# Two attention layers on a graph: the sums over keys leave TensorE, v's weights are streamed, and the order of work is rewritten

## The chip, the cores and the metric

The kernel runs on one NeuronCore of a Trainium2 chip. The metric is the device time of one execution in microseconds (us). Before the change it was 2666.83 us, the median of three runs (2666.81 to 2668.23).

The core has a matrix engine (TensorE, PE in the profile; its weight loads are PEld), three engines for elementwise work (VectorE is DVE, ScalarE is ACT, GpSimd is POOL) and a sync engine (SP), whose queue issues nearly all DMA transfers of this kernel. Each queue and each engine takes its instructions in order.

## The reference

There are 64 batches of 256 tokens with 512 features, and one 256 x 256 adjacency matrix for all. Everything is float32.

```python
# layer 0: masked attention, 8 heads of 64
q = (x @ Wq + bq).reshape(b, n, H, HD); k = (x @ Wk + bk)...; v = (x @ Wv + bv)...
scores = jnp.einsum('bqhd,bkhd->bhqk', q, k) / jnp.sqrt(jnp.float32(HD))
scores = scores + (1.0 - adj)[None, None, :, :] * -1000000000.0
attn = jax.nn.softmax(scores, axis=-1)
out = jnp.einsum('bhqk,bkhd->bqhd', attn, v).reshape(b, n, d)
x = _layernorm(x + (out @ Wo + bo), axis=-1)
# layer 1: graph attention from two projections of h
h = jnp.einsum('bnc,cf->bnf', x, W)
s1 = jnp.einsum('bnf,f->bn', h, a1); s2 = jnp.einsum('bnf,f->bn', h, a2)
e = jax.nn.leaky_relu(s1[:, :, None] + s2[:, None, :], negative_slope=ALPHA)
e = e * mask[None, :, :]                       # mask is adj
h_prime = jnp.einsum('bij,bjf->bif', jax.nn.softmax(e, axis=2), h)
x = _layernorm(x + jax.nn.elu(h_prime + beta * h), axis=-1)
```

## The kernel before, in words

**Tiling.** Batches go in pairs (`pair`, L619): 32 pairs, m = 0 to 31. A pair shares the projections q, k and v; all else is done by batch (`batch`, L702), s = 0 and 1 in the pair. A projection (`project`, L435) is done in quarters with seven products in place of eight (a Strassen scheme): the left side is a weight matrix with its sums, the right side the tokens with theirs (`token_sums`, L414, four subtractions on GpSimd). The seven products go to the PSUM tiles ps_chain, ps_cross, ps_second, ps_fourth or ps_pair, all at L455, in the order 1, 5, 2, 6, 3, 4, 7 for the wide ones.

The blocks of TensorE's work are named as the code names them, and the texts below use these names:

- **x**: transposing the input. **q, k, v**: projections of a pair, 7 products of 8 matmul records each.
- **scores** (S): per batch, 32 records on half the rows of the array, two head groups at once (ps_sc, L779). VectorE adds the mask (L786), ScalarE takes exp (L788), GpSimd adds the two key halves (L791, tile `both`), VectorE transposes in 32 x 32 blocks (L797, tile `flip`) and reduces (L798, tile `part`).
- **sums** (d): one matmul with `fold_sb` (ps_den, L806) ends the sum over keys over the partitions. Then VectorE inverts it (L809) and checks its range (L811), SP stores it to `rows` in DRAM (L815) and loads it spread over all partitions into `inv_all` (L820).
- **mix** (M): attention times v, 32 records on half the columns (ps_pv, L756); its result oT is multiplied by `inv_all` (L873).
- **o**: output projection, added to X (L951), then the norm (`norm`, L584: mean and square sums on ScalarE, three small operations on GpSimd, scaling on ScalarE, L608).
- **logits, attention**: the second layer's softmax, without TensorE for all but the last pair: dot products (L974), a transpose `svT` (L997), a store and a broadcast load (`line`, `row`, L998 and L1000), elementwise work (L1003 to L1023), a store `square` and four loads `att_b` (L1040, L1043), and a transpose (L1047) into attT.
- **spread** (y): attention times X (small products, 4 records each). **u**: projection of y, then elu, the second norm and the store of the result (`finish`, L715).

**Weights.** wq and wk are streamed (`streamed`, L380): the seven left sides are loaded for each pair, product by product, into six `piece` buffers of 256 KB. Wv, Wo and W stay in SBUF with their sums (`weight_sums`, L366, four operations on GpSimd).

**What sets the order.** The code doesn't issue instructions directly. It records operations with a cost, and `Plan.place` (L127) orders them on all engines from these costs, the lags of transfers and the number of buffers of each kind (`slots`, L258). TensorE's order is given by hand: `ROUND` lists the blocks of one round, `LATER` says how many rounds after its pair's number a block comes, and `FINISH` lists the end (`take_turn`, L612). At the end of TensorE's order the planner picks freely among the last 70 operations. A round is the work of one pair's length, with blocks of up to four pairs in it.

Of the kernel before, what the change touches and what calls it, by code (L numbers as in the profile page):

```python
# [16 lines left out]
P = 128  # L17
# [5 lines left out]
ROUND = ("v", "x", "spread1", "scores20", "scores00", "scores10", "scores30", "o1", "logits0", "q", "logits1", "u1",  # L23
         "sums0", "mix0", "scores11", "scores21", "scores01", "scores31", "attention0", "k", "spread0", "o0", "mix1",
         "sums1", "u0", "attention1")

LATER = {"x": -1, "v": 0, "spread1": 2, "scores20": 0, "scores10": 0, "scores30": 0, "scores00": 0, "o1": 1, "q": -1,
         "logits1": 1, "u1": 2, "sums0": 0, "mix0": 0, "scores11": 0, "scores21": 0, "scores01": 0, "scores31": 0,
         "attention0": 1, "k": -1, "spread0": 1, "o0": 0, "mix1": 0, "logits0": 1, "sums1": 0, "u0": 1, "attention1":
         1}  # L30

FINISH = (("scores20", 0), ("scores30", 0), ("logits0", 1), ("v", 0), ("spread1", 2), ("scores10", 0),
          ("attention0", 1), ("scores00", 0), ("u1", 2), ("o1", 1), ("sums0", 0), ("scores21", 0), ("mix0", 0),
          ("logits1", 1), ("spread0", 1), ("o0", 0), ("attention0", 0), ("spread1", 1), ("u1", 1), ("logits1", 0),
          ("attention1", 1), ("scores01", 0), ("u0", 1), ("logits0", 0), ("attention1", 0), ("spread0", 0), ("o1", 0),
          ("scores11", 0), ("u1", 0), ("sums1", 0), ("u0", 0), ("spread1", 0), ("scores31", 0), ("mix1", 0))
SAFE = 1e15

# [23 lines left out]
class Plan:  # L62
# [13 lines left out]
    SWITCH = {None: 100.0, "rows": 200.0, "columns": 100.0, "sums": 100.0, "one": 100.0}  # L76
# [50 lines left out]
    def place(self):  # L127
# [47 lines left out]
        while len(order) < len(ops):  # L175
            best = None
            for e, cand in ready.items():
# [3 lines left out]
                for n in cand:  # L181
# [18 lines left out]
                    if e == "PE" and ns:  # L200
                        cost = self.SWITCH[mode] if m != mode else self.AGAIN if start > now[e] else 0.0
# [8 lines left out]
            if e == "PE" and ns:  # L210
                start += self.SWITCH[mode] if m != mode else self.AGAIN if start > now[e] else 0.0
                mode = m
# [31 lines left out]
def gnn_two_layers(ctx: ExitStack, tc: tile.TileContext, x, adj, Wq, bq, Wk, bk, Wv, bv, Wo, bo, W, a, beta, out):  # L244
# [13 lines left out]
    slots = {"xin": 2, "x": 4, "two": 6, "xP": 1, "piece": 6, "full": 4, "half": 17, "flip": 1, "part": 1, "inv": 1,  # L258
             "xS": 2, "st": 72, "ps": 8, "rows": 4, "svT": 4, "line": 4, "square": 4}
# [37 lines left out]

    ident = const.tile([P, P], F32, name="ident")
# [19 lines left out]
    def by_partition(v, name):  # L318
        v_sb = const.tile([P, C], F32, name=name)
        with nc.allow_non_contiguous_dma(reason="one small vector, once"):  # L320
            nc.gpsimd.dma_start(v_sb, v.rearrange("(c p) -> p c", p=P))
        return v_sb

    def on_all(ap, offset, n, name):
        v_sb = const.tile([P, n], F32, name=name)
        nc.gpsimd.dma_start(v_sb, row_on_all(ap, offset, n))
        return v_sb

    wv_sb = weight(Wv, "wv_sb")
# [13 lines left out]
    fine_sb = once([32], "fine_sb")  # L343
    plan.op("POOL", 100, lambda: nc.gpsimd.memset(fine_sb[A], 1.0), [], [fine_sb])
    last_ok = st(1, "last_ok")
    fold_sb = once([32], "fold_sb")
    plan.op("DVE", 150, lambda: nc.vector.tensor_reduce(
        fold_sb[A], ident.rearrange("p (b j) -> p j b", j=32), AX.X, ALU.add), [], [fold_sb])
    maskT_sb = once([NT, N], "maskT_sb")

# [15 lines left out]
    def weight_sums(w, name, engine, reads=()):  # L366

        S = once([3, 2, F], name)
        eng, ns = (nc.vector, 700) if engine == "DVE" else (nc.gpsimd, 1300)
# [10 lines left out]
    def streamed(w, w_dram, name):  # L380
# [4 lines left out]
        for n, to, p, m, op, reads in ((1, s1, w21, w22, ALU.add, [w]), (2, s2, s1, w11, ALU.subtract, [w, S[1]]),  # L385
                                       (4, s4, w12, s2, ALU.subtract, [w, S[2]]), (3, s3, w11, w21, ALU.subtract, [w])):
            plan.op("DVE", 700, lambda to=to, p=p, m=m, op=op: nc.vector.tensor_tensor(to(), p(), m(), op), reads,  # L387
                    [S[n]])
# [25 lines left out]
    def token_sums(T, keys, name, width=P):  # L414
# [9 lines left out]
        def sub(dst, p, m, reads, writes):  # L424
            plan.op("POOL", 180 + 545 * width // P, lambda: nc.gpsimd.tensor_tensor(dst(), p(), m(), ALU.subtract),  # L425
                    reads, writes)
# [63 lines left out]
    def gather(quarter, bias=None, wide=False):  # L490

        def copy(q, acc):
# [4 lines left out]
            for f in range(2):  # L497
                plan.op("ACT", 470, lambda f=f: nc.scalar.activation(
                    dst()[:, f, :], src()[:, f, :], AF.Identity,
                    bias=bias[:, 2 * q[0] + f:2 * q[0] + f + 1]), [acc], [key])  # L500
# [37 lines left out]
    def residual_bias():  # L538
        bo_sb = for_now(bo, 0, "bo")
        acc, part = ps([D], "ps_b"), sb("half", [D], "bv_wo")  # L540
        for c in range(C):
# [3 lines left out]
                [(wo_sb, c)], [part], mode="two" if c else None)  # L545
# [10 lines left out]
    def second_layer_constants():  # L556
        plan.op("POOL", 500, lambda: nc.gpsimd.memset(diag_sb[A], 0.0), [w_sb], [diag_sb])
        for t in range(NT):
            plan.op("DVE", 250, lambda t=t: nc.vector.tensor_scalar(
                diag_sb[:, t, blk(t)], ident, beta_sb, None, ALU.mult), [], [diag_sb])  # L560
# [23 lines left out]
    def norm(X, ts):  # L584
# [10 lines left out]

        for i, t in enumerate(ts):
            total(i, t, 725, AF.Identity, mean, scale=-1.0 / D)
# [9 lines left out]
        for i, t in enumerate(ts):  # L607
            plan.op("ACT", 810, lambda i=i, t=t: nc.scalar.activation(  # L608
# [3 lines left out]
    def take_turn(m, what):  # L612
        at_end = (what, B // 2 - 1 - m) if m is not None else None
        if at_end in FINISH:
# [4 lines left out]
    def pair(m, at, general=False):  # L619
# [49 lines left out]
        right = token_sums(xT, lambda k, j: [(xT, (j, s)) for s in range(2)], "xS", N)  # L669
# [6 lines left out]
        if m == 0:  # L676
            wq_sb, wk_sb = sb("two", [C, D], "wq_sb"), sb("two", [C, D], "wk_sb")
            load(wq_sb, Wq)
            load(wk_sb, Wk)
            lq, left["q"] = streamed(wq_sb, Wq, "wq_sums")  # L680
# [3 lines left out]
            plan.turn = (plan.turn[0], plan.turn[1] + 0.5)  # L684
# [3 lines left out]
            left["v"] = weight_sums(wv_sb, "sv_sb", "POOL")  # L688
            plan.turn = (0, ROUND.index("x"))
# [7 lines left out]
        project(left["v"], right, False, [V], *gather(  # L697
# [4 lines left out]
    def batch(m, s, qT, kT, V, dram, general):  # L702
# [12 lines left out]
        def finish(ts, us, u, mode):  # L715

            for t in ts:
# [461 lines left out]
```

## Time and profile before

| | |
|---|---|
| median of three runs | 2666.83 us |
| the profiled execution, its own time | 2666.57 us |
| its span, first to last instruction | 2664.8 us |
| granted TensorE clock, mean | 0.998 |
| TensorE busy | 2643.7 us (99%) |
| VectorE, GpSimd, ScalarE busy | 1999.7, 1637.5, 1550.5 us |
| DMA | 300.70 MB, mean 113 GB/s, queue of SP 42.1% of 16 engines |

How to read the timeline's lines: start in us from the span's beginning, length, engine, line of the code, operation, output<-inputs, rows*columns of the array in use, shape, number of records; in brackets the idle time of the engine before it and what ended it. A record's length contains its way through the array, so the next one starts before it ends: durations on TensorE are taken from start to start. In the list of waits a line says who waited for whom, the total in us, the number of times, and the longest.

### The profile page before, as it was taken

What the parts mean: (1) busy time and instruction counts of PE and PEld (TensorE: products, weight loads), DVE (VectorE), ACT (ScalarE), POOL (GpSimd) and SP (SyncE); (2) the same over time, 40 slices, a digit from 0 to 9 for tenths busy, and PEclk for the clock granted to TensorE, in tenths of its full rate; (3) what the DMA queues carried; (4) which work ended last, traced back from release to release, by engine and by line L of the source; (5) the groups of instructions that cost most, each with busy time, mean ns of one, the idle gap of its engine ahead of it and who ended that gap; (6) DMA issues with size and microseconds to landing.
All of it is one profiled execution on the core that took longest, in us unless ns stands there. A gap on an engine that the chain in (4) does not pass through costs nothing.

```text
span 2664.8 us, 45965 instructions
## 1 busy us (share of the span) xinstructions
PE 2643.7 (99%) x15037; PEld 2288.5 (86%) x15037; DVE 1999.7 (75%) x4053; ACT 1550.5 (58%) x3585; POOL 1637.5 (61%) x2255
## 2 busy tenths in 40 slices
PE   9999999999999999999999999999999999999998
PEld 7888888888888888888888888888888888888886
DVE  6677787777877777777778777787777777777876
ACT  3456565555655565655656555565556565565666
POOL 4665665655756556566566565575655656656655
PEclk9999999999999999999999999999999999999999
DMA  8343443444534434444344344453443444444321
GB/s 253 83 104 111 124 127 92 114 116 112 132 95 114 116 109 124 109 108 109 112 123 127 92 113 117 113 131 96 114 117 108 125 109 106 109 113 123 96 64 53
DMA packets 583084, 300.70 MB, mean 113 GB/s; under 512 B 409400, under 2 KB 513848, under 8 KB 582840
## 3 DMA queue, kind: packets, MB, share of 16 engines
q1 hardware_dynamic: 582712, 297.68, 42.1%
q8 instruction: 123, 2.02, 0.3%
q14 instruction: 121, 0.99, 0.1%
q0 software_dynamic: 128, 0.01, 0.0%
HBM read 245.11 MB, written 52.48 MB: 112 GB/s over the span
## 4 chain that ended last, share of the span: by engine, by line
PE 98%; DVE 0%; ACT 0%; DMA 0%; SPq 0%; issue 0%; POOL 0%; ACTq 0%; DVEq 0%
PE ps_chain L455 35%; PE ps_cross L455 23%; PE ps_sc L779 9%; PE ps_pv L756 9%; PE ps_pair L455 8%; PE ps_fourth L455 7%; PE ps_second L455 7%; PE ps_den L806 0%; DMA wq_sb<-in_L_gnn_Wq_dram 0%; ACT junk L591 0%; PE ps_plain L523 0%; DVE wq_sums_s L387 0%; DVE oT L873 0%; PE ps_y L1058 0%; PE ps_plain L518 0%; PE ps_plain L520 0%
## 5 line engine op out<-in xcount | busy, mean ns | idle before, releaser
L791 POOL TENSOR_TENSOR both<-pT 128x256 f32<-128x256 f32 x504 | 361.3, 742 | 55.9 <-ACT pT L788 55.8
L788 ACT ACTIVATE pT<-pT 128x512 f32<-128x512 f32 x512 | 307.0, 627 | 104.6 <-DVE pT L786 102.2
L602 POOL TENSOR_SCALAR rs<-sq 128x2 f32<-128x2 f32 (+1 forms) x130 | 25.4, 195 | 537.5 <-ACT junk L591 534.6
L591 ACT ACTIVATE junk<-x 128x512 f32<-128x512 f32 x256 | 159.7, 624 | 330.1 <-DVE x L951 311.8
L786 DVE TENSOR_TENSOR pT<-ps_sc,maskT_sb 128x512 f32<-128x512 f32 x512 | 319.7, 682 | 38.3 <-PE ps_sc L779 37.8
L1083 POOL TENSOR_TENSOR X_sums<-x 128x256 f32<-128x256 f32 x126 | 126.3, 1012 | 284.0 <-DVE x L720 211.6
L779 PE MATMUL ps_sc<-qT,kT 64*128 64x256 f32 x2048 | 240.2, 383 | 0.0
L756 PE MATMUL ps_pv<-pT,v 128*64 128x256 f32 x2048 | 238.1, 382 | 0.0
L779 PEld LDWEIGHTS ps_sc<-qT,kT 64*128 64x128 f32 x2048 | 193.2, 187 | 37.4 <-issue 12.2
L608 ACT ACTIVATE x<-x,nmr,rs 128x512 f32<-128x512 f32 x256 | 200.3, 807 | 31.5 <-POOL nmr L604 31.5
L756 PEld LDWEIGHTS ps_pv<-pT,v 128*64 128x64 f32 x2048 | 175.7, 137 | 44.3 <-issue 10.7
L974 DVE SCALAR_TENSOR_TENSOR junk<-x,wa_sb 128x512 f32<-128x512 f32 x256 | 173.9, 691 | 46.7 <-ACT x L608 46.6
L591 ACT ACTIVATE junk<-x,mean 128x512 f32<-128x512 f32 x256 | 182.8, 714 | 2.0
L797 DVE STREAM_TRANSPOSE flip<-both 128x512 f32<-128x512 f32 x252 | 176.8, 702 | 7.0 <-POOL both L791 0.5
L798 DVE TENSOR_REDUCE part<-flip 128x16 f32<-128x512 f32 x252 | 170.2, 676 | 3.2
L740 POOL TENSOR_TENSOR x<-x,res_sb 128x512 f32<-128x512 f32 x128 | 160.8, 1278 | 0.9 <-DMA x<-in_x_dram 0.9
L455 PE MATMUL ps_chain<-so_sb,oS 128*128 128x256 f32 x504 | 129.4, 379 | 0.0
L455 PE MATMUL ps_chain<-sw_sb,yS 128*128 128x256 f32 x504 | 129.4, 379 | 0.0
L951 DVE TENSOR_TENSOR x<-x,ps_chain 128x256 f32<-128x256 f32 x252 | 100.8, 411 | 28.9 <-PE ps_chain L455 27.8
L455 PE MATMUL ps_chain<-sv_sb,xS 128*128 128x256 f32 x512 | 120.9, 379 | 0.0
L425 POOL TENSOR_TENSOR oS<-oT 128x256 f32<-128x256 f32 x126 | 101.2, 803 | 30.8 <-DVE oT L873 23.1
L455 PE MATMUL ps_chain<-xS,wk_sums 128*128 128x256 f32 x496 | 117.2, 379 | 0.0
(246 smaller groups left out, 6985.2 us busy)
## 6 DMA issues: line engine op xcount, KB each, us to landing
x<-in_x_dram SPq DMA_DIRECT2D x64, 512.0 KB, 5.2
out_dram<-x SPq DMA_DIRECT2D x128, 256.0 KB, 2.9
inv_all<-rows SPq DMA_DIRECT2D x126, 256.0 KB, 4.1
xin<-in_x_dram SPq DMA_DIRECT2D x248, 128.0 KB, 3.2
wq_sums<-wq_sums SPq DMA_DIRECT2D x124, 256.0 KB, 3.4
wk_sums<-wk_sums SPq DMA_DIRECT2D x124, 256.0 KB, 2.6
wq_sums<-in_L_gnn_Wq_dram SPq DMA_DIRECT2D x93, 256.0 KB, 2.9
wk_sums<-in_L_gnn_Wk_dram SPq DMA_DIRECT2D x93, 256.0 KB, 2.7
```

The costliest lines, as they stand in the source:

```text
L455: nc.tensor.matmul(dst[:, f, :], lhs, rhs, start=start and f == 0 and c == 0, stop=c == inner - 1, skip_group_check=True)
L591: plan.op("ACT", ns, lambda: nc.scalar.activation(junk[A], X[:, t, :], func, accum_out=to[:, i:i + 1], **{k: v() if callable(v) else v for ...
L608: plan.op("ACT", 810, lambda i=i, t=t: nc.scalar.activation(X[:, t, :], X[:, t, :], AF.Identity, bias=nm[:, i:i + 1], scale=rs[:, i:i + 1] ...
L740: plan.op("POOL", 1300, lambda t=t: nc.gpsimd.tensor_tensor(X[:, t, :], X[:, t, :], res_sb[A], ALU.add), [res_sb], tokens(t))
L756: nc.tensor.matmul(acc[r * HD:(r + 1) * HD, i, :], V[:, 2 * k + s, h * HD:(h + 1) * HD], pT[h][:, k, :], start=k == 0, stop=k == NT - 1)
L779: nc.tensor.matmul(acc[j][:, k, :], kT[r:r + HD, c, key_blk(k)], own(qT, r, c), start=True, stop=True)
L786: plan.op("DVE", 680, lambda h=h, i=i: nc.vector.tensor_add(pT[h][A], acc[i][A], maskT_sb[A]), [acc[i], maskT_sb], [pT[h]])
L788: plan.op("ACT", 620, lambda h=h: nc.scalar.activation(pT[h][A], pT[h][A], AF.Exp, scale=1.0 / HD ** 0.5), [pT[h]], [pT[h]])
L791: plan.op("POOL", 735, lambda h=h, i=i: nc.gpsimd.tensor_tensor(both[c][:, i, :], pT[h][:, 0, :], pT[h][:, 1, :], ALU.add), [pT[h]], [(bot ...
L797: plan.op("DVE", 700, lambda: nc.vector.transpose(turned[A], both[c][A]), [both[c]], [turned])
L798: plan.op("DVE", 685, lambda: nc.vector.tensor_reduce(part[:, 2 * c:2 * c + 2, :], turned[A].rearrange("p i (q k) -> p i q k", k=32), AX.X ...
L974: plan.op("DVE", 770, lambda t=t, i=i, junk=junk: nc.vector.scalar_tensor_tensor(junk[A], X[:, t, :], 1.0, wa_sb[:, i, :], op0=ALU.mult, o ...
```

## The change

- `denominators` has no matmul. Four SP transfers bring the four groups of 32 partitions of `part` beside each other into `four` (a buffer of the kind `flip`), VectorE reduces over the four, inverts, checks the range, and transposes, and the store to `rows` follows. `fold_sb` is gone. The block sums no longer exists; for the last batch it takes its turn with mix.
- v is streamed like q and k: seven loads for each pair. `wv_sb` and its sums don't stay in SBUF. Buffers: half 17 to 23, piece 6 to 7, svT 4 to 3.
- The costs of a change of the array's shape in the planner are new and go by the mode that is entered.
- `ROUND`, `LATER` and `FINISH` are new: o comes two rounds after its pair's number, y and u three. `START` writes out the first blocks of pairs 0 and 1. Three matmuls on a constant (`busy`) stand ahead of everything.
- For the first pair the token sums are on VectorE. The small loads of biases and beta become recorded operations. [...]
- In the last pair the second norm's mean comes from an accumulator of VectorE's last addition, and its scaling is on VectorE.

```diff
-ROUND = ("v", "x", "spread1", "scores20", "scores00", "scores10", "scores30", "o1", "logits0", "q", "logits1", "u1",
-         "sums0", "mix0", "scores11", "scores21", "scores01", "scores31", "attention0", "k", "spread0", "o0", "mix1",
-         "sums1", "u0", "attention1")
+ROUND = ("spread0", "scores21", "scores11", "scores01", "scores31", "mix0", "x", "logits1", "k", "o0", "u0", "mix1",
+         "attention1", "scores00", "scores10", "scores20", "scores30", "logits0", "v", "attention0", "spread1", "o1",
+         "u1", "q")
...
+LATER = {"scores00": 1, "scores10": 1, "scores20": 1, "scores30": 1, "scores21": 2, "scores11": 2, "scores01": 2,
+         "scores31": 2, "q": 0, "spread0": 3, "mix0": 2, "x": 0, "k": 1, "o0": 2, "u0": 3, "mix1": 2, "attention1": 3,
+         "logits0": 2, "v": 0, "logits1": 2, "attention0": 2, "spread1": 3, "o1": 2, "u1": 3}
...
+START = (("x", 1), ("x", 0), ("q", 0), ("k", 0), ("mask", 0), ("v", 0), ("scores20", 0), ("scores30", 0),
+         ("scores10", 0), ("scores00", 0), ("q", 1), ("consts", 0), ("bias", 0), ("v", 1))
...
-    SWITCH = {None: 100.0, "rows": 200.0, "columns": 100.0, "sums": 100.0, "one": 100.0}
+    SWITCH = {None: 200.0, "rows": 190.0, "columns": 137.0, "sums": 137.0}
...
-    slots = {"xin": 2, "x": 4, "two": 6, "xP": 1, "piece": 6, "full": 4, "half": 17, "flip": 1, "part": 1, "inv": 1,
-             "xS": 2, "st": 72, "ps": 8, "rows": 4, "svT": 4, "line": 4, "square": 4}
+    slots = {"xin": 2, "x": 4, "two": 6, "xP": 1, "piece": 7, "full": 4, "half": 23, "flip": 1, "part": 1, "inv": 1,
+             "xS": 2, "st": 72, "ps": 8, "rows": 4, "svT": 3, "line": 4, "square": 4}
...
+    def busy(n):
+        acc = ps([F], "ps_warm")
+        def pe():
+            for _ in range(n):
+                nc.tensor.matmul(acc[A], warm.to_broadcast([P, P]), warm.to_broadcast([P, F]), start=True, stop=True)
+        plan.op("PE", 864 * n, pe, [], [acc])
+    plan.turn = (-10, 0)
+    busy(3)
...
-        right = token_sums(xT, lambda k, j: [(xT, (j, s)) for s in range(2)], "xS", N)
+        right = token_sums(xT, lambda k, j: [(xT, (j, s)) for s in range(2)], "xS", N, "POOL" if m else "DVE")
...
-            left["v"] = weight_sums(wv_sb, "sv_sb", "POOL")
-            plan.turn = (0, ROUND.index("x"))
+            lv, left["v"] = streamed(wv_sb, Wv, "wv_sums")
+            turn("bias")
...
-            norm(X, ts)
+            norm(X, ts, sums)
...
-                turn("sums")
-                acc, inv = ps([32], "ps_den"), sb("inv", [32], "inv")
-                plan.op("PE", 80, lambda: nc.tensor.matmul(
-                    acc[0:P // 2], part[A].rearrange("p h q -> p (h q)"), fold_sb[A], start=True,
-                    stop=True), [part, fold_sb], [acc], mode="one", claims=[inv])
-                plan.op("DVE", 342, lambda: nc.vector.reciprocal(inv[0:P // 2], acc[0:P // 2]), [acc], [inv])
+                W, four = P // 4, sb("flip", [2, N], "four")
+                inv = sb("inv", [P // 2], "inv")
+                def gathered():
+                    return four[0:W, 0, :].rearrange("n (b c) -> n b c", b=4)
+                def fold():
+                    for b in range(4):
+                        nc.sync.dma_start(gathered()[:, b, :], part[b * W:(b + 1) * W].rearrange("n h q -> n (h q)"))
+                plan.op("SP", 1720, fold, [part], [(four, 0)], lag=2400)
+                plan.op("DVE", 330, lambda: nc.vector.tensor_reduce(
+                    inv[0:W], gathered().rearrange("n b c -> n c b"), AX.X, ALU.add), [(four, 0)], [inv])
+                plan.op("DVE", 200, lambda: nc.vector.reciprocal(inv[0:W], inv[0:W]), [], [inv])
...
+                plan.op("DVE", 160, lambda: nc.vector.transpose(four[0:W, 1, 0:P // 2], inv[0:W]), [inv], [(four, 1)])
```

## The prediction

> **What bounds the kernel now.** First the page: busy time, the clock and the chain that ended last.
>
> ```profile
> PE 2643.7 (99%) x15037; PEld 2288.5 (86%) x15037; DVE 1999.7 (75%) x4053; ACT 1550.5 (58%) x3585; POOL 1637.5 (61%) x2255
> PEclk9999999999999999999999999999999999999999
> PE 98%; DVE 0%; ACT 0%; DMA 0%; SPq 0%; issue 0%; POOL 0%; ACTq 0%; DVEq 0%
> ```
>
> TensorE is the chain, at full clock, so only what shortens its own line of work, or holes in it, can move the end. A busy share can't tell work from slow passages, so I read TensorE's timeline of one round next, start to start.
>
> ```profile
> 1204.42 3.72 PE L779 MATMUL ps_sc<-qT,kT 64*128 64x256 f32 x32
> 1208.08 1.99 PE L455 MATMUL ps_chain<-xT,wk_sums 128*128 128x256 f32 x8
> 1209.91 1.89 PE L455 MATMUL ps_cross<-xT,wk_sums 128*128 128x256 f32 x8
> 1211.64 1.89 PE L455 MATMUL ps_second<-xT,wk_sums 128*128 128x256 f32 x8
> ...
> 1229.53 3.67 PE L756 MATMUL ps_pv<-pT,v 128*64 128x256 f32 x32
> 1233.04 0.25 PE L806 MATMUL ps_den<-fold_sb,part 128*64 128x32 f32 x2
> 1233.22 1.13 PE L455 MATMUL ps_chain<-w_sb,yT 128*128 128x256 f32 x4
> ...
> 1286.41 3.72 PE L779 MATMUL ps_sc<-qT,kT 64*128 64x256 f32 x32
> ```
>
> One round (a pair of batches) is 1286.41 - 1204.42 = 81.99 us, with no idle entry. A plain product is 1211.64 - 1209.91 = 1.73 us, but the first one after the scores is 1209.91 - 1208.08 = 1.83. Changes of the array's shape cost time inside "busy".
>
> The holes are in the first 100 us:
>
> ```profile
> 8.41 3.36 PE L455 MATMUL ps_chain<-xT,wq_sb 128*128 128x256 f32 x8
> 15.97 1.97 PE L455 MATMUL ps_chain<-xS,wq_sums_s 128*128 128x256 f32 x8 [0.75 <-DVE wq_sums_s L387]
> 86.41 1.10 PE L455 MATMUL ps_chain<-wo_sb,oT 128*128 128x256 f32 x4 [0.56 <-DVE oT L873]
> 89.72 2.00 PE L455 MATMUL ps_cross<-wo_sb,oT 128*128 128x256 f32 x4 [2.21 <-POOL oT L425]
> 90.00:93.00 3.00, 3.00 (x8) 2.37 (x8) 0.42 (x1) 0.00 (x0) 1.19 (x2) 0.50 0.00 0
> ```
>
> The last line is the sum over a stretch; its 0.50 is the granted clock, so the wait for the first o's token sums is paid twice, idle and then at half clock.
>
> **The change part by part.**
>
> *TensorE's line.* Round before, from the built order: v y S o q u d M S k y o M d u (S scores, M mix, d the one-matmul ps_den). Round after: q y S M k o u M S v y o u. The products are the same: 21 of 1.727, 28 of 0.8635, 14 of 0.446, 4 S or M of 3.455 (16 full 0.216 us, as half-array matmuls run in twos) = 80.51 us. The rest of 81.99, 1.47 us, is shape changes. Priced: an S block takes 3.655, 0.20 over; an M block without ps_den (one near the end) 3.60, 0.145 over; a plain block after S or M 0.105 more, before one 0.093 more (0.309 for the last matmul instead of 0.216). M, two ps_den matmuls and the way to u take 1233.22 - 1229.53 = 3.69, so ps_den adds 0.09; the one ahead of M adds 0.12. Check: 2 x 0.20 + 2 x 0.145 + 3 x 0.105 + 3 x 0.093 + 0.21 = 1.49 against 1.47. After: 2 x 0.20 + 2 x 0.145 + 2 x 0.105 + 2 x 0.093 = 1.09, a round of 81.6, **0.39 us less**. Start and finish differ too, so I count the whole order: 294 shape changes before, 200 after. S and M entries are alike (130 and 131, +0.2). Plain blocks entered from S, M or d, and left for one: 99 and 99 before, 68 and 68 after: -31 x 0.198 = -6.1. 63 ps_den: -63 x 0.105 = -6.6. Together **-12.5 us**.
>
> *Sums over keys without TensorE.* Each of the 63 batches gains four 8 KB SBUF transfers, a reduction (0.33 us by the 0.34 of today's reciprocal of like size), a transpose (0.16) and loses the matmul. No SBUF to SBUF transfer is in the trace; nearest is the 8 KB store of the inverses, 1.7 us from issue to landing; I take 2.1 (square<-e) and bound it by 1.7 and 3.4. With four issues of 0.45 the way from part to the stored row grows by about 4.5 us. It lies beside TensorE: scores to inv_all is 10 (adds, exps, flips) + 3.9 + 0.9 + 2.2 + 5.4 = 22.4 us, and the multiplication that needs it comes behind the mix: 50 us after the scores of a pair's first batch (v y o u q y S M), 31 after the second's (M k o u M). The transfers stand on SP in front of later pieces of weights, whose users are 10 us off or more. Cost 0; without that cover 4.5 us each. VectorE gains 0.35 us a batch, 62.6 of 82 us.
>
> *v streamed.* Seven pieces of 256 KB in 31 pairs: +57 MB on 300.7, the DMA share goes from 42% to 50%. A piece's slot comes free seven products earlier; the shortest gap between two streamed blocks, q to k, is y + S + M = 10.5 us, against 0.4 of issue and 3.4 to land. Cost 0; a landing over 10 us would be needed. The buffers (half 17 to 23, piece 7) let S and M of different batches stand side by side; they cost nothing themselves.
>
> *Start.* Three warm matmuls fill TensorE ahead of the first transfer's landing at 3.75. Today the clock rises only at 11.3: the first product takes 3.20 instead of 1.73, and 0.9 is lost before 15.97. But wq's second half lands only at 10.98 (VectorE's first wq sum starts then), so products 1 and 2 end at 10.98 + 1.73 = 12.7 at best. VectorE, with four token sums (0.65 each, done by 11.4) ahead of wq's, has s1 at 12.0 and s2 at 13.3, as needed, and five more products end q at 12.7 + 5 x 1.73 = 21.35 instead of 22.95, **-1.6** (bounds -2.5 and 0, if VectorE's sums stay at the 1.6 us that they take today while GpSimd works on token sums too). The small loads on GpSimd's queue (0.55 to 0.97 an issue) become planned steps; their users start at 11.8, so they cost nothing. The mask, row and ps_b keep their lengths and change places; wo's load goes behind q's pieces on SP, and its first user, the bias, stands behind the second q. v's weight sums leave GpSimd (4 x 1.6) and a whole v block now stands ahead of the first o: GpSimd's o sums are ready 3 us early, so 0.73 + 2.37 idle and 1.77 of half clock go, **-4.9** (bounds -4.9 and -1). But the first y now follows its o after M S v o q, 37.6 us; before it was 56.7. On VectorE that batch's dot products stand behind v's fifth product. Counted from v: dots and transpose 12.4, line 2.5 to 14.9, row 3.4 to 18.3, z, leaky and mask 23, exp and scale 24.6; square waits on SP behind q's fourth piece, 25.1 + 2.6 = 27.7; four att_b issues and landing 5.2, 32.9; transpose 33.6. TensorE wants it at 30.3: 3 us idle. **A rule and a row differ here.** Above, waits of 0.73 and 2.37 us brought 3.4 us at clock 0.50. The Trainium skill, "TensorE: Matmul & The Clock Gate", The HAM clock gate, says the array falls to half rate after an idle window of about 3.4 us and then needs as long to warm. By the rule a 3 us hole costs 3.0, by the row 3.0 + 1.7; the row decides: **+4.5** (bounds 0 and 9).
>
> *Finish.* The last pair's mean comes from VectorE's accumulator and its scaling moves there. Today the last matmul ends at 2652.0 and the last scale at 2659.1, with ScalarE's queue full. After: final exp at +1.5 to 2.1 behind others, add 2.9, mean 3.4, square 4.4, GpSimd's 1.1 to 5.6, scale 6.1 instead of 7.1: **-1.0**. The new final order has the second to last batch's o 22.8 us after its scores, where the longer sums path needs about 22.4 and then its token sums: **+1.5** (0 to 4).
>
> Sum: -12.5 - 1.6 - 4.9 + 4.5 - 1.0 + 1.5 = **-14.0**. The profiled execution took 2666.57 (span 2664.8, 1.8 outside it), 0.3 below the median of 2666.83. So 2666.8 - 14.0 = **2653**.
>
> **The rivals.**
>
> *The softmax chain sets the round (slower).* From the o to the y of a pair's first batch there were 79 us; now 53. Unqueued the chain is 33 us (norm and dots 9.6, line and row 6.3, softmax 6.6, square 2.5, att_b 5.2, transpose and sums 3). Followed through the new order, with the dots behind scores, flips and oT and SP's line behind a piece that TensorE frees, attT is ready 2.5 us before y. For it: today's chain is served lazily and no later round waits, but the next line shows why SP is fragile: it waits in order.
>
> ```profile
> SPq L1040 <- DVE e L1023: 261.9, 61, 13.9
> SPq L998 <- DVE svT L997: 254.0, 59, 12.2
> ```
>
> Beyond 2.5 us of lateness each further us costs 27 full rounds 27 us; past 3.0 us it eats the gain. At 1 us over: 2653 + 27 = 2680. Against it: today attT also comes only 2 to 3 us ahead, by choice of priority, and nothing waits.
>
> *Pieces of v late.* Needs landings past 10 us; the median is 3.4 at 42% DMA share. At 1 us a round, 2680 again.
>
> *No net change.* The line shrinks, but start and finish lose as much: 5 us more at the first y, 4 at the finish, and 0.1 us a round: about 2665.
>
> *All start waits vanish:* 4.5 + 1.5 less, with a warmer q: 2646.
>
> **How the numbers follow.** Likeliest case 0.66, its own range 2648 to 2659. All waits gone 0.08. A lesser gain that still counts 0.04. No net change 0.08. Chain or pieces late 0.14. A measurement tells 0.2%, 5.3 us, from no change, so below 2661.5 is faster: 0.78, within 0.08, slower 0.14. The range 2645 to 2668 leaves out the late rounds and little of the rest.
>
> **What would show it.** Right: rounds of 81.6 us start to start without ps_den; M 3.60 after S; no idle before the first o; a wait of about 3 us on attT at the first y, with a stretch of clock 0.50; last scale 6 us after the last matmul. Wrong: idle entries in every round before ps_chain<-attT,x or ps_cross<-w_sb,yT, or before a product that waits for a piece; a q block as slow as today's.

## The result, and the profile after

The changed kernel takes 2767.1 us (median of 4 runs, 2761.64 to 2769.82) against 2667.44 beside it: ratio 1.0371, 95% interval [1.0353, 1.0389]. That is 100 us slower, where 14 us faster was forecast. The profiled execution took 2769.82, its span is 2768.1. Two single executions lie far off the others of their kernel, 3070.61 us of the kernel before and 8239.33 us of the one with eight transfers, and are left out of the times and ratios below.

From the page of the changed kernel: busy time, the clock in tenths, the SyncE queue's DMA, and the chain that ended last.

```profile
PE 2674.5 (97%) x14917; PEld 2263.6 (82%) x14917; DVE 2107.8 (76%) x4198; ACT 1532.5 (55%) x3573; POOL 1656.2 (60%) x2247
PEclk9999999999999999999999999999999999999999
q1 hardware_dynamic: 638536, 357.71, 50.3%
DVE 0%; issue 0%
```

These lines say little. TensorE's share falls from 99% to 97%, the clock row shows only nines although the mean granted clock fell from 0.998 to 0.986, and the chain breaks off after two instructions, so it names no bound. The DMA share is the 50% that was forecast. The list of waits says more. TensorE's three longest and the fold's on VectorE, with columns waited for, us in total, times, longest:

```profile
PE ps_cross L480 <- DVE x L1005: 60.9, 28, 3.7
PE ps_chain L480 <- DVE attT L1101: 7.7, 1, 7.7
PE ps_chain L480 <- DVE x L1005: 7.0, 6, 4.6
...
DVE inv L859 <- DMA four<-part: 98.5, 44, 6.4
```

TensorE waits in 28 rounds for VectorE's addition `x` (L1005), which takes a product of o out of the accumulator. VectorE itself waits 44 times for `four`, the fold. One round shows how the two belong together. TensorE's timeline, the o of a pair's first batch:

```profile
1034.80 1.03 PE L480 MATMUL ps_chain<-wo_sb,oT 128*128 128x256 f32 x4
1035.66 1.03 PE L480 MATMUL ps_cross<-wo_sb,oT 128*128 128x256 f32 x4
1036.53 1.03 PE L480 MATMUL ps_pair<-wo_sb,oT 128*128 128x256 f32 x4
1037.39 1.03 PE L480 MATMUL ps_chain<-so_sb,oS 128*128 128x256 f32 x4
1041.00 2.07 PE L480 MATMUL ps_cross<-so_sb,oT 128*128 128x256 f32 x4 [2.58 <-DVE x L1005]
1042.87 1.80 PE L480 MATMUL ps_pair<-wo_sb,oS 128*128 128x256 f32 x4
...
1037.39:1045.37 7.98, 5.39 (x17) 0.79 0.38 105
```

The fifth product goes into `ps_cross`, the accumulator of the second, and may start only when VectorE has added the second to x. It starts 2.58 us late and then runs at half clock: 2.07 us instead of 1.03. The last line is the sum over that stretch: its length, TensorE's busy time and matmuls, the granted clock, 0.79, and the DMA's share and GB/s. VectorE at the same time:

```profile
1035.00 1.29 DVE L529 TENSOR_TENSOR kT<-ps_chain,kT 128x512 f32<-128x512 f32 x2
1036.21 0.41 DVE L1005 TENSOR_TENSOR x<-x,ps_chain 128x256 f32<-128x256 f32 x1
1036.53 0.16 DVE L1074 RECIPROCAL rc<-sm 128x2 f32<-128x2 f32 x1
1040.04 0.57 DVE L859 TENSOR_REDUCE inv<-four 32x64 f32<-32x256 f32 x1 [3.35 <-DMA four<-part]
1040.55 0.40 DVE L1005 TENSOR_TENSOR x<-x,ps_cross 128x256 f32<-128x256 f32 x1
1040.88 0.53 DVE L861 RECIPROCAL inv<-inv 32x64 f32<-32x64 f32 x1
```

The reduction over the fold stands behind o's first addition and ahead of all the others. Its data land 3.35 us later, and the addition that TensorE needs, ready since the second product ended, waits in line behind it. SyncE's queue in the same round shows why the fold is late:

```profile
1030.85 0.69 DVE L842 TENSOR_REDUCE part<-flip 128x16 f32<-128x512 f32 x1
...
1025.10 0.62 SPq L427 DMA_DIRECT2D wv_sums<-in_L_gnn_Wv_dram  x1
...
1027.12 1.14 SPq L432 DMA_DIRECT2D wv_sums<-wv_sums  x1
...
1029.70 1.11 SPq L427 DMA_DIRECT2D wv_sums<-in_L_gnn_Wv_dram  x1
1030.86 1.29 SPq L692 DMA_DIRECT2D xin<-in_x_dram  x2
1032.25 1.29 SPq L432 DMA_DIRECT2D wv_sums<-wv_sums  x1
1033.59 0.58 SPq L692 DMA_DIRECT2D xin<-in_x_dram  x1
1034.27 0.83 SPq L432 DMA_DIRECT2D wv_sums<-wv_sums  x1
1035.20 2.47 SPq L856 DMA_DIRECT2D four<-part  x4
```

(The first line is VectorE's.) The last `part` is written at 1031.54. The four transfers are issued only from 1035.20 on, behind loads of the next x and pieces of v, and the reduction starts 2.96 us after the start of the last issue. Over all pairs, for the first batch, the medians are 3.75 us from data to first issue, 1.88 from the start of the first issue to the start of the last, and 2.15 from there to the reduction. For the second batch they are 0.16, 1.91 and 2.96, and there the reduction stands behind three of o's additions.

I add up TensorE's start-to-start times over the whole trace. A pause is idle where the next matmul starts more than 0.28 us later than its length; slow is what matmuls at about half clock took over their length. Start is the first 175 us, finish the last 210 us ahead of the last matmul.

| kernel | start: idle, slow | rounds: idle, slow | finish: idle, slow | time |
|---|---|---|---|---|
| before | 5.1, 5.0 | 0, 2.6 | 0.4, 0.9 | 2666.8 |
| changed | 15.1, 6.4 | 71.6, 27.9 | 7.5, 1.6 | 2767.1 |

In the rounds, 65.4 us of the idle time are the 28 stalls at o's fifth product (counted start to start; the list of waits has 60.9). In the kernel before the clock is full in all rounds, so some 2.6 us of the slow time there are not the clock's. The rest of the loss lies in the start and in the finish.

### The profile page after: what moved, and what is told of

Read it like the earlier page. It is cut to its first block, busy times and chain, and to the rows that moved or that the text cites. A ratio compares the mean times of both kernels' runs of the same rounds, so it can differ in the third digit from the quotient of the medians.

```text
span 2768.1 us, 46536 instructions
## 1 busy us (share of the span) xinstructions
PE 2674.5 (97%) x14917; PEld 2263.6 (82%) x14917; DVE 2107.8 (76%) x4198; ACT 1532.5 (55%) x3573; POOL 1656.2 (60%) x2247
## 3 DMA queue, kind: packets, MB, share of 16 engines
q1 hardware_dynamic: 638536, 357.71, 50.3%
q14 instruction: 126, 1.03, 0.1%
## 5 line engine op out<-in xcount | busy, mean ns | idle before, releaser
L835 POOL TENSOR_TENSOR both<-pT 128x256 f32<-128x256 f32 x504 | 373.6, 764 | 41.0 <-ACT pT L832 38.9
L451 POOL TENSOR_TENSOR yS<-yT 128x256 f32<-128x256 f32 x126 | 91.8, 729 | 212.1 <-DVE yT L529 182.6
L800 PEld LDWEIGHTS ps_pv<-pT,v 128*64 128x64 f32 x2048 | 141.4, 137 | 85.6 <-issue 11.3
L1028 DVE SCALAR_TENSOR_TENSOR junk<-x,wa_sb 128x512 f32<-128x512 f32 x256 | 193.6, 774 | 1.2
L1137 POOL TENSOR_TENSOR X_sums<-x 128x256 f32<-128x256 f32 x126 | 110.9, 896 | 124.8 <-ACT m L761 86.0
L451 POOL TENSOR_TENSOR oS<-oT 128x256 f32<-128x256 f32 x126 | 112.4, 892 | 114.2 <-DVE oT L927 109.5
L480 PE MATMUL ps_chain<-so_sb,oS 128*128 128x256 f32 x504 | 135.9, 394 | 7.1 <-DVE x L1005 7.0
L1057 ACT ACTIVATE z<-row,s 128x256 f32<-128x256 f32 x124 | 56.4, 501 | 146.1 <-DMA row<-line 111.1
L480 PE MATMUL ps_cross<-so_sb,oT 128*128 128x256 f32 x252 | 77.6, 436 | 60.9 <-DVE x L1005 60.9
```

The lines of the kernel that those rows point to most:

```text
L451: plan.op(engine, ns, lambda: eng.tensor_tensor(dst(), p(), m(), ALU.subtract), reads, writes, mode="two")
L480: nc.tensor.matmul(dst[:, f, :], lhs, rhs, start=start and f == 0 and c == 0, stop=c == inner - 1, skip_group_check=True)
L800: nc.tensor.matmul(acc[r * HD:(r + 1) * HD, i, :], V[:, 2 * k + s, h * HD:(h + 1) * HD], pT[h][:, k, :], start=k == 0, stop=k == NT - 1)
L835: plan.op("POOL", 735, lambda h=h, i=i: nc.gpsimd.tensor_tensor(both[c][:, i, :], pT[h][:, 0, :], pT[h][:, 1, :], ALU.add), [pT[h]], [(bot ...
L1028: plan.op("DVE", 770, lambda t=t, i=i, junk=junk: nc.vector.scalar_tensor_tensor(junk[A], X[:, t, :], 1.0, wa_sb[:, i, :], op0=ALU.mult, o ...
```

## The experiments

Theory A: the place of the reduction on VectorE, ahead of o's additions, makes the fold's landing a wait of TensorE. Theory B: the fold would be in time for that place if SyncE were not behind. Rival C: neither; the shorter softmax chain, v's pieces or the DMA load slow every round.

**The reduction placed later.** The planner takes its arrival to be 5 us later. SyncE's order in the rounds stays but for one issue of `square` in each.

```
-                plan.op("SP", 1720, fold, [part], [(four, 0)], lag=2400)
+                plan.op("SP", 1720, fold, [part], [(four, 0)], lag=2400, late=5000)
...
-                    base[u] = max(base[u], start + ns + self._lag(n, u))
+                    base[u] = max(base[u], start + ns + self._lag(n, u) + self.late[n])
```

> The changed kernel, with one thing altered in the planner: it places the reduction over the four folded pieces 5 us later on VectorE than the arrival it assumes, so that the reduction stands behind six of o's adds in a pair's first batch and behind all of them in the second, instead of behind one and three. SyncE's order stays. Theory A (VectorE waits for the fold's landing with o's adds queued behind it): the stalls between o's products go, 65 us of idle in 28 rounds and 5 us at the first o, with some 27 us of half clock after them; about 2670. Rival C (the shorter softmax chain, v's pieces or the DMA load slow every round): the time stays near 2767.

2675.06 us, ratio to before 1.0033 [1.0021, 1.0046]. VectorE's timeline of this run (its lines stand two lower in the code):

```profile
992.70 0.42 DVE L1007 TENSOR_TENSOR x<-x,ps_pair 128x256 f32<-128x256 f32 x1 [0.44 <-PE ps_pair L482]
993.04 0.57 DVE L861 TENSOR_REDUCE inv<-four 32x64 f32<-32x256 f32 x1
993.56 0.42 DVE L1007 TENSOR_TENSOR x<-x,ps_chain 128x256 f32<-128x256 f32 x1
```

The reduction now finds its data landed, although they still wait 3.73 us on SyncE, and VectorE waits for TensorE instead. No round has an idle entry (0 idle and 2.9 slow in the rounds). Most rounds take 81.596 us, the longest of those in the middle 81.94. Theory A holds and C falls: 92 us go with the place of the reduction and of the few operations on its result. But 2675 is not 2653. The start still has 9.0 us of idle time, 7.0 of them at the first y, and the finish has 17.8.

**The fold on ScalarE's queue.** The reduction stays ahead of all but one of o's additions. The planner counts 0.30 us on ScalarE for the four issues.

```
-                        nc.sync.dma_start(gathered()[:, b, :], part[b * W:(b + 1) * W] ...)
+                        nc.scalar.dma_start(gathered()[:, b, :], part[b * W:(b + 1) * W] ...)
...
-                plan.op("SP", 1720, fold, [part], [(four, 0)], lag=2400)
+                plan.op("ACT", 300, fold, [part], [(four, 0)], lag=3800)
```

> The changed kernel with the four fold transfers issued from ScalarE's queue instead of SyncE's; the reduction stays where it is, ahead of o's adds. Theory B (the fold's data wait 3.75 us on SyncE behind pieces of v and x, as the trace shows for a pair's first batch): issued at once the fold lands some 3.5 us earlier, the stall of 2.4 us (median) goes, about 2670. Theory A alone (the transfers themselves land too late for the place of the reduction): no change, about 2767.

2772.73 us, ratio 1.04 [1.0382, 1.0419], as slow as the changed kernel, but for another reason. TensorE's longest wait, a line of TensorE and two of ScalarE:

```profile
PE ps_cross L480 <- ACT yT L520: 54.7, 28, 2.8
...
215.36 0.71 PE L480 MATMUL ps_cross<-attT,X_sums 128*128 128x128 f32 x4 [1.83 <-ACT yT L520]
...
212.45 2.44 ACTq L856 DMA_DIRECT2D four<-part  x4
214.94 0.37 ACT L520 COPY yT<-ps_cross 128x256 f32<-128x256 f32 x1 [2.78 <-issue]
```

The fold is now issued 0.03 us after its data, and the stalls in o are gone: theory B's half of the mechanism holds. The number was missed, because the four issues hold ScalarE for 2.44 us and its copies of a y stand behind them. Again there are 28 stalls, now at y. An issue holds the engine that makes it, here for 2.44 us in four; the plan had it as nearly free.

**The sums on TensorE again.** One `ps_den` matmul ahead of each mix, as before; nothing else.

> The changed kernel with the sums over keys ended by TensorE again (one ps_den matmul ahead of each mix), all else kept. Theories A and B: the stalls in o go as no VectorE instruction waits for a fold; 63 ps_den cost 63 x 0.105 = 7 us and some more shape changes; about 2676 to 2685. Rival C: no better than 2767, as the chain, v's pieces and the order stay.

2690.91 us, ratio 1.0098 [1.0082, 1.0115]. The stalls in o are gone (1.4 us idle in the rounds), as A and B say and C does not. Undisturbed rounds take 81.816 us, 0.22 more than 81.596, so two `ps_den` cost 0.22 against the 2 x 0.105 of the prediction. The total missed its range by 6 us: the last 70 operations of TensorE, which the planner orders freely, came out with 19.7 us of idle time, 9.9 of it at one o. It is therefore no measure of what the transfers gain.

**The kernel before with the transfers alone.** Its order, resident v and buffers stay (a slot of `svT` goes, to make room).

> The kernel before with only the sums over keys moved to transfers and VectorE; its order, its resident v and its buffers stay. The reduction comes to stand ahead of all of o's adds in one batch and between q's in the other. Theory A (the place on VectorE is enough): stalls there, 1 to 2 us a batch and the slow clock after them, 2700 to 2760. Theory B (it takes v's pieces on SyncE ahead of the fold as well): no stall, 63 ps_den less, 2667 - 7 = 2660.

2781.05 us, ratio 1.0432 [1.0415, 1.045]: worse than theory A's range, and B's 2660 falls. No v is on SyncE here, the fold is issued 0.39 and 0.03 us after its data, and still every round stalls. The first two lines are the waits on VectorE and TensorE; the others are timelines of VectorE, ScalarE and TensorE:

```profile
DVE oT L880 <- DMA inv_all<-rows: 64.9, 20, 5.1
...
PE ps_chain L452 <- ACT u L492: 39.4, 30, 1.5
...
1026.05 1.47 DVE L880 TENSOR_TENSOR oT<-oT,inv_all 128x512 f32<-128x512 f32 x2 [2.71 <-DMA inv_all<-rows]
...
1029.81 0.35 ACT L492 COPY u<-ps_chain 128x256 f32<-128x256 f32 x1
...
1030.30 1.10 PE L452 MATMUL ps_chain<-sw_sb,yS 128*128 128x256 f32 x4 [1.36 <-ACT u L492]
```

In the old order the inverses are needed sooner after the scores than the longer path delivers them. VectorE waits up to 5.1 us for `inv_all`, and o's additions also stand behind the reduction. ScalarE's norm starts late (its sums wait for `x`), its copies of u stand behind the norm, and TensorE waits at u in two places, 30 times each, 1.3 and 0.8 us on average; 90.0 us are idle in the rounds. So the longer path was not hidden in the old order either. The wait that shows it is another than the changed kernel's, so this run is no clean test of A against B. The new order does give `inv_all` its cover: in the changed kernel VectorE waits for it once, 0.6 us. What the new order did not cover is the reduction itself.

**SyncE's issues priced as they take.** In the changed kernel a piece of v takes 0.62 us (raw) or 0.78 us (a stored sum) to issue, medians, where the pieces of q and k take 0.38 and 0.33; the planner counts 0.43 and 0.37. Here it counts 0.85, and for the fold's four issues 1.90 instead of 1.72.

```
-                plan.op("SP", 430, lambda: nc.sync.dma_start(
+                plan.op("SP", 850, lambda: nc.sync.dma_start(
...
-                plan.op("SP", 370, lambda: nc.sync.dma_start(piece[A].rearrange("p c f -> p (c f)"), kept[k - 1]),
+                plan.op("SP", 850, lambda: nc.sync.dma_start(piece[A].rearrange("p c f -> p (c f)"), kept[k - 1]),
...
-                plan.op("SP", 1720, fold, [part], [(four, 0)], lag=2400)
+                plan.op("SP", 1900, fold, [part], [(four, 0)], lag=2400)
```

> The changed kernel, with the planner's cost of an issue of a piece of a streamed weight raised from 0.43 and 0.37 us to 0.85, near what v's pieces take beside the loads of x (0.62 and 0.78 us median, up to 1.4). On VectorE the reduction stays ahead of all but one of o's adds; on SyncE the fold moves ahead of some of v's and x's issues. Theory B (the fold is late because SyncE is behind the planner's clock): the fold issues within 1 us of its data, most of the 65 us of stalls in o and the half clock after them go: 2667 to 2680. Theory A alone (a place ahead of o's adds stalls whatever SyncE does): near 2767.

2676.74 us, ratio 1.0036 [1.0021, 1.005]: theory B's value, with the reduction still ahead of all but one of o's additions. The medians for the first batch's fold are now 1.33 us to the first issue, and 5.9 us of idle time are left in the rounds. From SyncE's and VectorE's timelines of one round:

```profile
991.56 0.58 SPq L692 DMA_DIRECT2D xin<-in_x_dram  x1
992.24 3.36 SPq L856 DMA_DIRECT2D four<-part  x4
995.70 0.53 SPq L432 DMA_DIRECT2D wv_sums<-wv_sums  x1
...
996.89 0.58 DVE L859 TENSOR_REDUCE inv<-four 32x64 f32<-32x256 f32 x1 [0.80 <-DMA four<-part]
```

The fold goes ahead of v's last pieces and the last loads of x. VectorE waits 0.80 us here instead of 3.35, which the gap between o's products mostly hides. So A and B are two halves of one cause: the place chosen on VectorE was right for the planner's SyncE and wrong for the real one, and either correction alone removes some 90 us of the loss. This run changes the orders of VectorE, ScalarE and GpSimd a little as well. It mends SyncE's clock, not v's streaming itself; the changed order with v resident was not run. (In the old order, with v resident, the fold was issued 0.39 and 0.03 us after its data.)

**The later place, but not at the end.** The reduction is placed 5 us later except in the last three pairs.

```
-                plan.op("SP", 1720, fold, [part], [(four, 0)], lag=2400)
+                plan.op("SP", 1720, fold, [part], [(four, 0)], lag=2400,
+                        late=5000.0 if m is not None and m < B // 2 - 3 else 0.0)
```

> As the run with the reduction placed 5 us later, but not in the last three pairs, so that the finish is planned as in the changed kernel. The later place cost that run 17.8 us of idle at the finish against 7.5 in the changed kernel. Theory: rounds of 81.6 us, finish as in the changed kernel: 2675 - 10 = 2665, just at the time before. If the finish stays as slow: 2675.

2661.94 us (20 runs), ratio to before 0.9983 [0.9976, 0.9989]: the one version that is faster than the kernel before by more than the interval, by 5 us. TensorE's order is that of the changed kernel, and in the rounds only the reduction with the operations on its result, one small operation of VectorE and one issue of `square` change their places. All rounds in the middle take 81.595 or 81.596 us. The finish has 7.2 us of idle time, as in the changed kernel.

**Two turns moved for the first y and for a late u.**

```
+        elif (what, m) == ("spread0", 0):
+            plan.turn = (LATER[what], ROUND.index("mix0") + 0.5)
...
-          ("spread1", 2), ("u1", 2), ...
+          ("spread1", 2), ("o1", 1), ("u1", 2), ...
```

(In the second place the o stood ahead of the y.)

> As the run before it (later place of the reduction but for the last three pairs), and two turns on TensorE changed: the first y stands behind the scores and the mix that followed it (7.3 us more cover for its 7 to 8 us wait), and in the finish the y of the second to last pair's second batch stands ahead of an o instead of directly ahead of its own u. Theory (the start's and the finish's waits are what is left of the loss): 8 us at the first y and 5 at that u less, about 2652. If other waits take their place: 2660 to 2665.

2664.97 us, ratio 0.9994 [0.9985, 1.0003]: the second case, other waits in their place. TensorE's line at the first y:

```profile
154.36 1.19 PE L482 MATMUL ps_chain<-att_sums,X_sums 128*128 128x128 f32 x4 [5.43 <-ACT yT L522]
```

attT is there in time now, but y's fourth product waits for ScalarE's copy of the first, which stands in ScalarE's line behind exponentials, z and copies of oT. The finish keeps 7.1 us of idle time, spread over other products, and the tail after the last matmul grows from 9.5 to 13.8 us. Moving a turn re-orders the plan behind it.

**Eight transfers for four,** of half the size, planned at the old cost.

```
-                        nc.sync.dma_start(gathered()[:, b, :], part[b * W:(b + 1) * W]...)
+                        for w in range(0, W, W // 2):
+                            nc.sync.dma_start(gathered()[w:w + W // 2, b, :],
+                                              part[b * W + w:b * W + w + W // 2]...)
```

> The changed kernel with the fold in eight transfers of half the size instead of four, planned at the old cost, so that every engine's order stays: SyncE issues 4 x 0.47 = 1.9 us longer. Theories A and B: the reduction waits 1.9 us longer in 28 rounds, 53 us more, and more of the stalls bring the half clock: 2820 to 2850. Rival C (the loss is not this wait): 2767 to 2775.

2904.37 us (three runs), ratio 1.0882 [1.086, 1.0903], past the range. Every engine's order of work is that of the changed kernel. TensorE's two longest waits:

```profile
PE ps_cross L480 <- DVE x L1007: 121.4, 28, 5.7
PE ps_chain L480 <- DVE x L1007: 39.3, 30, 6.6
```

The stalls of the first batch grow from 65.4 to 125.9 us, 2.16 each. The 1.9 of the forecast came from 0.47 us an issue; from the first start to the last the issues take 4.40 us instead of 1.88, 2.5 more, so an issue takes 0.63. What I had left out is the second batch: there the reduction had come just in time, and now it stalls too, 28 times and 36.7 us in all. Slow time rises from 27.9 to 59.3. The time follows the fold's lateness and has no slack left on either batch.

**Both corrections together, and then the first y moved as well.**

> The later place of the reduction (but for the last three pairs) and the raised cost of the pieces' issues together; TensorE's order as in the changed kernel. With the raised costs alone the first y waited 4.8 us instead of 7.2. Theory (stalls in o are gone by the first alone, the second only brings the first y's transfers forward): 2662 - 2.4 = 2659.5. If the new order of SyncE's queue costs something elsewhere: 2664 or more.

> As the run before it, with the first y behind the scores and the mix that followed it. There it waited for 5.4 us in its fourth product for ScalarE's copy of its own first product, which stands in ScalarE's line where the planner expected that product later. If the order on ScalarE stays as the planner sees it: the same wait, 2659 to 2662. If the earlier transfers let it find its place: 2655.

2665.32 us, ratio 0.9993 [0.9985, 1.0002], and 2665.36, 0.9996 [0.9987, 1.0004]. Neither improves on the later place alone. With both, small waits of 0.3 to 0.8 us return at u in some rounds (2.1 us in all), and the first y waits 6.4 us instead of 4.8. With y moved, it waits 5.0 us in its fourth product, the same wait as in the run with two turns moved. My expectations for the start missed in both.

**The u of the finish behind two scores.**

```
-          ("spread1", 2), ("u1", 2), ("scores31", 0), ("scores21", 0), ("mix0", 0), ...
+          ("spread1", 2), ("scores31", 0), ("scores21", 0), ("u1", 2), ("mix0", 0), ...
```

> As the run with the later place but for the last three pairs, and one turn of the finish moved: two of the score products come between the y of the second to last pair's second batch and its u, which there waited 3.46 us for GpSimd's sums of that y and then ran at half clock for 1.3. Theory: 2 us of cover, the half clock gone as well, 3 us less: 2659. If the planner's free order of the last 70 products changes for the worse: 2662 to 2670.

2669.43 us, ratio 1.0008 [0.9999, 1.0017]: the second case. That u waits 0.88 us instead of 3.46, but the free order of the last products comes out with 12.6 us of idle time in the finish instead of 7.2.

The same sums as above, for the runs that were not shown there:

| kernel | start: idle, slow | rounds: idle, slow | finish: idle, slow | time |
|---|---|---|---|---|
| reduction later | 9.0, 5.6 | 0, 2.9 | 17.8, 3.1 | 2675.1 |
| issues priced | 8.6, 6.4 | 5.9, 7.0 | 7.5, 2.9 | 2676.7 |
| later but for the end | 11.9, 6.0 | 0, 2.6 | 7.2, 1.9 | 2661.9 |
| eight transfers | 16.3, 7.0 | 170.4, 59.3 | 10.5, 3.1 | 2904.4 |

## Why the prediction was wrong

**The step that failed is "Sums over keys without TensorE", cost 0.** Its duration was right: from the first issue to the reduction 1.88 + 2.15 = 4.0 us where the reduction waits, against 3.9. (An issue takes 0.63 us, not 0.45, but the landing counts from the start of the last one.) Its cover was right too: `inv_all` is in time for its multiplication. What it never asked is who stands behind the new wait. It followed the fold's data to their user, found 31 to 50 us of room, and stopped there. The reduction on VectorE is an instruction that waits, with seven of o's eight additions in line behind it, and once o's second product is done TensorE can run only two more before it needs that product's addition. The step should have read in VectorE's built order where the reduction stands, and compared its arrival with the additions behind it.

**The second half of the same step.** "The transfers stand on SP in front of later pieces of weights" is the reverse of what happens in a pair's first batch: they stand behind pieces of v and loads of x, 3.75 us. This is where **v streamed, cost 0** failed as well. It looked at the pieces' landing (right: no product waits for one) and at the DMA share (right: 50.3%), and took an issue as 0.4 us. In the round shown, five pieces of v stand between the loads of x ahead of the fold, and take 0.62 + 1.14 + 1.11 + 1.29 + 0.83 = 4.99 us, where the planner counts 2 x 0.43 + 3 x 0.37 = 1.97. That is 3.0 us more, beside the 3.66 us from the fold's data to its first issue.

**TensorE's line, -12.5, was right where it could be read, in the rounds.** The round came out at 81.596 us once nothing waited (forecast 81.6), M at 3.60 after S (3.60), `ps_den` at 0.11 each (0.105).

**Start.** q ends at 21.56 (forecast 21.35): -1.4 for -1.6. VectorE's sums of two inputs take 0.69 us there; they took 1.6 before, while GpSimd made sums at the same time. The first o was to lose its stall; its token sums are in time, but it stalled 4.6 us for the reduction. With the later place that stall is gone, so the -4.9 stands for the order itself. The first y was sized at 4.5 and bounded at 9. In the changed kernel:

```profile
141.32 0.38 SPq L1094 DMA_DIRECT2D square<-e  x1
142.21 0.32 SPq L432 DMA_DIRECT2D wk_sums<-wk_sums  x1
146.80 2.63 SPq L1097 DMA_DIRECT2D att_b<-square  x4
...
153.38 1.22 PE L480 MATMUL ps_chain<-attT,x 128*128 128x128 f32 x4 [7.75 <-DVE attT L1101]
```

The walk had `square` issued 25.1 us after v's start (here 115.15), and it was 26.2. It gave the landing 2.6 us including the issue, from today's median, and it took 146.80 - 141.32 = 5.5. The four issues of att_b and their landing took 146.80 to 152.62, 0.6 longer than the walk's 5.2. The idle time is 7.9 us for 3, the slow clock after it 1.9 for 1.7 (this y takes 5.13 us instead of 3.22): 9.8 for 4.5. This wait doesn't decide between the rule and the row that the prediction set against each other, as 7.75 us is more than the rule's 3.4 too. The stalls in o do: 2.58 us were enough in the round shown.

**Finish.** The tail is shorter by more than forecast: from the last matmul to the end of the span 2768.1 - 2757.85 = 10.25 us against 12.8, -2.5 for -1.0. The last scaling ends 5.4 us after the last matmul (forecast 6.1, before 7.1), and what follows it is 0.9 us shorter. The final order costs 7.5 idle and 1.6 slow against 0.4 and 0.9 before, +7.8 for +1.5. I had followed one o, but the longest wait is another:

```profile
2673.73 2.51 POOL L784 TENSOR_TENSOR x<-x,res_sb 128x512 f32<-128x512 f32 x2
2676.19 0.73 POOL L451 TENSOR_TENSOR yS<-yT 128x256 f32<-128x256 f32 x1
...
2679.44 2.07 PE L480 MATMUL ps_cross<-w_sb,yT 128*128 128x256 f32 x4 [3.29 <-POOL yT L451]
```

This u follows its own y directly, and GpSimd's sums of that y stand behind other additions.

**The sum with measured terms,** the stalls in o left out and the start and finish taken from the changed kernel: -12.5 - 1.4 - 4.9 + 9.8 + 7.8 - 2.5 = -3.7, so 2666.8 - 3.7 = 2663.1. The version without those stalls measured 2661.94. Even with the fold harmless the forecast of 2653 would have been 9 us too low, all of it from the first y and the finish.

**The rivals.** The softmax chain and late pieces of v, the two slow ones, didn't happen: no round waits for attT or for a piece. The observation about SyncE that stood with the first of them, that it waits in order and is fragile, was the right one, but was applied to the wrong transfer.

## What to carry to other kernels

Where a change adds a wait, look up what stands behind the waiting instruction on its own engine before asking when its result is needed; one reduction of 0.57 us, placed five additions too early in a pair's first batch, cost some 90 us. A static plan is as good as its price of an issue: here an issue of 0.4 us in the plan took 0.6 to 0.8 on the queue, and mending either the price or the place removed most of the loss. A plan that orders its end freely re-orders it for every small edit (7 to 20 us of idle time at the finish in these runs), so compare the rounds and the ends separately.

## What was not expected of the hardware

Short waits bring the half clock, depending on their length. In four of these runs (the changed kernel, ScalarE's queue, the transfers alone, the eight transfers), 87 stalls of TensorE between 1.0 and 1.75 us were followed by half clock once, and there another wait had just preceded. Of 53 stalls from 1.75 to 3.25 us, 39 were followed by it, and of 40 longer ones all. After such a stall some six to thirteen matmuls take twice their time (427 ns instead of 216 for the 256-column ones), 1.3 us and more. The transfers alone waited 90 us in the rounds with a mean clock of 0.998, because their stalls are short.

Which of the middle stalls bring it can be read from the traces as well. In all thirteen, the granted clock changes only at points 3.41 us apart, the same ones through a whole trace. Here are two such stretches of the round shown above (the columns are those of the sum over a stretch above):

```profile
1037.61:1041.02 3.41, 0.83 (x5) 1.00 0.59 153
1041.02:1044.43 3.41, 3.41 (x8) 0.50 0.07 21
```

In the first TensorE stands idle for 2.58 us, and the second has half clock. Leaving out the first 25 us, the thirteen traces hold 10045 stretches at full clock. In 105 of them TensorE stood idle for more than 1.8 us, and 96 of these were followed by half clock; of the other 9940 one was. So what counts in these runs is the idle time inside one stretch, a little over half of it, and a stall of 2 us that two stretches share can pass. The Trainium skill, "TensorE: Matmul & The Clock Gate", The HAM clock gate, puts the fall after an idle window of about 3.4 us that runs freely. The length and the free running agree with these traces; that the whole window must be idle doesn't, and there the measurement decides.

An issue from SyncE is not of fixed length: pieces of the same 256 KB take 0.33 to 0.38 us for q and k and 0.62 to 0.78 for v, whose pieces stand between the loads of x (medians; 1.29 in a line shown above, 2.93 at the most). Directly behind a load of x, v's pieces take 0.77 (raw) and 1.07 us (a stored sum); in the last pair, which has no loads of a next x beside it, they take 0.32 to 0.53. Why the loads do this is not shown by these runs.
